# Two additions of a convolution–attention kernel: GpSimd tensor adds replaced by accumulating on-chip transfers that GpSimd issues

## The chip, the cores and the metric

One Trainium2 chip, one of its cores. The metric is the device time of one execution of the whole kernel in microseconds (us). Inputs come from the chip's memory (HBM) and the result goes back there; between them the data stay in the on-chip memory (SBUF) and in the matmul accumulators (PSUM).

## The reference

The input x has 16 images of 256 channels and 56x56 pixels, in float32. Two layers follow one another, each with a residual:

```python
# layer 0, on the group-normalised x
xq = sign(gn(x) + bias)
out = 0
for i, d in enumerate((1, 3, 5)):                      # dilations
    y = grouped_conv3x3(xq, binarised(w[i]), dilation=d) + cb[i] - move1[i]
    out = out + where(y >= 0, y, alpha[i] * y) + move2[i]   # PReLU
x = x + layer_norm_over_channels(out) * gamma + beta   # first residual
# layer 1, on the group-normalised x: local attention over 3x3 neighbours
q, k, v = gn(x) @ qkv_w.T + qkv_b
...
x = x + proj(softmax(q * k) * v)                       # second residual
```

Two additions in it matter here: the one that adds the third dilation's PReLU to the sum of the first two, and the first residual.

## The kernel before, in words

**Tiling.** The 256 channels are four groups (g) of 64. A tile's 128 partitions hold 64 channels twice, once for each half of the image. An image is worked on in two units (u = 0, 1), each of 2x7 rows of 56 pixels in either half, so that a unit's tile for one group has 128 partitions of 2x392 float32, 784 elements, 3136 bytes on each partition and 401,408 bytes (392 KB) in all. One image therefore has 8 such tiles, 24 convolutions (8 tiles, three dilations each), 8 additions of the third dilation and 8 additions of the first residual; 16 images have 128 of either addition.

**Convolution** (`conv`, from L634). TensorE makes 36 matmuls into a PSUM tile (L644); there are four such PSUM tiles for the whole kernel. PReLU is written as alpha*y + (1 - alpha)*relu(y). For the first dilation ScalarE writes the linear part to the tile `ct` (L663); for the second, VectorE adds it to `ct` (L673); for the third (`POOLED = (2,)`), ScalarE writes it to a tile of its own, `rl` (L670). Then, for each, ScalarE takes the relu in PSUM (L678), and VectorE adds its share to `ct` or to `rl` (L683). Last, for the third dilation alone, GpSimd adds `rl` to `ct` (L689). There are seven `ct` tiles but a single `rl` tile (`kind("rl", UNIT, 1)`, L415): the next third dilation's L670 can't start before the addition at L689 has read `rl`.

**Channel norm and first residual** (`channel_norm`, from L721). ScalarE squares `ct` (L727), TensorE sums over channels (L697), small VectorE and ScalarE operations make mean and root (L741 to L749), VectorE subtracts the mean (L755) and scales (L765). Then GpSimd adds `ct` to the input tile `xt` (L778), and ScalarE squares the new `xt` with a running sum (L782), for which it uses `ct` as its output. After the four groups of both units, `fold` makes the group norm of layer 1 out of these sums (matmul L514, then L526 and on) and folds it into the projection's weights (L803, L825); `qkv` (L862) uses them.

**Attention.** GpSimd multiplies q and k for nine shifts (L915), TensorE sums (L937), a softmax follows (L950 to L972), TensorE spreads the weights (L986), VectorE multiplies by v (L997) and GpSimd adds up the nine terms (L1010); TensorE projects (L1027), VectorE makes the second residual (L1037), and the tile is stored.

**Transfers.** All are issued by SyncE (SP): halves of images for the statistics and the signs (`xh`, L544), the units' inputs (`xt`, L1202), results (`out`, L1047), and small copies between the two halves of the partitions (`sgn`, L606 and L607). GpSimd issues none.

**Order.** Every operation is handed to `Plan.op` with what it reads and writes. A table (`ORDER`) gives each a place in time, and `Plan.emit` issues them in that order, as soon as what an operation depends on has been issued and its buffers are to be had. So each engine has a fixed order of instructions, in which convolutions of the next image are mixed with attention of the one before, and an engine whose next instruction waits does nothing else. `pool(...)` puts an operation on GpSimd. `either(...)` does so too, but moves those that `ON_VECTOR` lists to VectorE; of the two additions these are three of the last image's residual additions (`"scale1$": (1, 4, 10)`). The place in the order is the same for `pool` and `either`.

Of the kernel before, what the change touches and what calls it, by code (L numbers as in the profile page):

```python
# [11 lines left out]
ALU = mybir.AluOpType  # L12
# [281 lines left out]
class Plan:  # L294
# [16 lines left out]
    def op(self, engine, emit, r=(), w=(), hold=(), engines=()):  # L311


        k = self.noted.get((self.stage, self.image), 0)
        self.noted[self.stage, self.image] = k + 1
        if engines:
            emit = partial(emit, engines[k in ON_VECTOR.get(self.stage, ())])
        bufs = [k[0] if isinstance(k, tuple) else k for k in (*r, *w, *hold)]
        bufs = [k for k in dict.fromkeys(bufs) if isinstance(k, Buf)]
        o = Op(PERIOD * self.image + ORDER[self.stage][k], emit, bufs)  # L320
        for b in bufs:
            if not b.left and b.kind in self.queues:
                self.queues[b.kind].append(b)
            b.left += 1
        before = {}
        for k in r:
            for x in self.wrote.get(k, ()):
                before[id(x)] = x
        for k in w:
            for x in (*self.wrote.get(k, ()), *self.read.get(k, ())):  # L330
                before[id(x)] = x
        for k in r:
            self.read.setdefault(k, []).append(o)
        for k in w:
            self.wrote[k], self.read[k] = [o], []
        for x in before.values():
            x.after.append(o)
            o.wait += 1
        self.ops.append(o)
# [35 lines left out]
def preact_conv_attention(  # L375
# [16 lines left out]
    nc = tc.nc  # L392
# [84 lines left out]
    def pe(f, r, w, hold=()):  # L477
        op("PE", f, r, w, hold)

    def act(f, r, w):  # L480
        op("ACT", f, r, w)

    def dve(f, r, w):
        op("DVE", f, r, w)

    def pool(f, r, w):
        op("POOL", f, r, w)
# [4 lines left out]
    def either(f, r, w):  # L492

        op("POOL", f, r, w, engines=(nc.gpsimd, nc.vector))
# [139 lines left out]
    def conv(b, u, g, d, ct):  # L634

        dil = DIL[d]
        ps = Buf("ps")

        def products():
            for tap in range(9):  # L640
                c0 = PADC + (tap % 3 - 1) * dil
                for h, q in ((0, 0), (1, 1), (0, 1), (1, 0)):
                    r0 = PADC + q * XR + u * SR + (tap // 3 - 1) * dil
                    nc.tensor.matmul(  # L644
                        out=ps[q * GC : (q + 1) * GC, h, 0:SN],
                        lhsT=wconv[h * GC : (h + 1) * GC, g, d, tap, :],
                        rhs=sgn[g][h * GC : (h + 1) * GC, r0 : r0 + SR, c0 : c0 + W],
                        start=tap == 0,
                        stop=tap == 8,
                    )  # L650


        pe(products, [("sgn", g), ("halo", g), ("wconv", g, d)], [ps], [ct])

        def n():
            return ps[:, :, 0:SN]

        s = slice(d, d + 1)

        to = Buf("rl") if d in POOLED else ct  # L660
        if d == 0:
            act(
                lambda: nc.scalar.activation(  # L663
                    ct.tile, n(), AF.Identity, bias=mv2[:, g : g + 1], scale=asc[:, g, s]
                ),
                [ps, ("scales", g, d), "mv2"],
                [ct],
            )
        elif d in POOLED:
            act(lambda: nc.scalar.mul(to.tile, n(), asc[:, g, s]), [ps, ("scales", g, d)], [to])  # L670
        else:
            dve(
                lambda: nc.vector.scalar_tensor_tensor(ct.tile, n(), asc[:, g, s], ct.tile, ALU.mult, ALU.add),  # L673
                [ps, ("scales", g, d)],
                [ct],
            )
        act(
            lambda: nc.scalar.activation(n(), n(), AF.Relu, bias=cbi[:, g, s], scale=csc[:, g, s]),  # L678
            [("scales", g, d)],
            [ps],  # L680
        )
        dve(
            lambda: nc.vector.scalar_tensor_tensor(to.tile, n(), oalpha[:, g, s], to.tile, ALU.mult, ALU.add),  # L683
            [ps],
            [to],
        )
        if d in POOLED:
            either(
                lambda e: e.tensor_tensor(ct.tile, ct.tile, to.tile, ALU.add),  # L689
                [to],  # L690
                [ct])


    def lanes_sum(ps, bank, src, g):

        for i in range(NVB):
            nc.tensor.matmul(  # L697
                out=ps[i * LANES : (i + 1) * LANES, bank, 0:VB],
                lhsT=cm32,
                rhs=src[:, i // 2, i % 2 * VB : (i % 2 + 1) * VB],  # L700
                start=g == 0,
                stop=g == NG - 1,
            )
# [17 lines left out]
    def channel_norm(b, u, ct, xt, sums):  # L721

        ps = Buf("ps")
        for g in range(NG):
            plan.at(f"var{u}", b)
            sq = Buf("sq")
            act(lambda g=g, sq=sq: nc.scalar.activation(sq.tile, ct[g].tile, AF.Square), [ct[g]], [sq])  # L727

            def sum_of_both(g=g, sq=sq):
                lanes_sum(ps, 0, ct[g], g)  # L730
                lanes_sum(ps, 1, sq, g)

            pe(sum_of_both, [ct[g], sq], [ps])
        plan.at(f"root{u}", b)
        ms, t, s, r = (Buf("lv") for _ in range(4))


        mean, square = (lambda i=i: ps[:, i, 0:VB] for i in range(2))
        tt = nc.vector.tensor_tensor
        stt = nc.vector.scalar_tensor_tensor  # L740
        act(lambda: nc.scalar.copy(ms.tile, mean()), [ps], [ms])  # L741
        dve(lambda: tt(t.tile, mean(), ms.tile, ALU.mult), [ps, ms], [t])
        dve(lambda: stt(mean(), t.tile, -1.0, square(), ALU.mult, ALU.add), [t], [ps])
        dve(lambda: nc.vector.tensor_scalar(mean(), mean(), 0.0, EPS_LN, ALU.max, ALU.add), [], [ps])
        act(lambda: nc.scalar.activation(t.tile, mean(), AF.Ln), [ps], [t])
        act(lambda: nc.scalar.activation(square(), t.tile, AF.Exp, scale=-0.5), [t], [ps])
        act(lambda: nc.scalar.activation(s.tile, square(), AF.Square, scale=0.5**0.5), [ps], [s])
        dve(lambda: stt(t.tile, mean(), -1.0, s.tile, ALU.mult, ALU.mult), [ps, s], [t])
        dve(lambda: stt(r.tile, t.tile, 1.5, square(), ALU.add, ALU.mult), [t, ps], [r])  # L749
        plan.at(f"mean{u}", b)  # L750
        mb = Buf("ps")
        lanes_spread(mb, ms)
        for g in range(NG):
            dve(
                lambda g=g: nc.vector.tensor_tensor(ct[g].tile, ct[g].tile, mb[:, :, 0:SN], ALU.subtract),  # L755
                [mb],
                [ct[g]],
            )
        plan.at(f"root{u}", b)
        rb = Buf("ps")  # L760
        lanes_spread(rb, r)
        for g in range(NG):
            plan.at(f"scale{u}", b)
            dve(
                lambda g=g: nc.vector.scalar_tensor_tensor(  # L765
                    ct[g].tile,
                    ct[g].tile,
                    gam[:, g : g + 1],
                    rb[:, :, 0:SN],
                    ALU.mult,  # L770
                    ALU.mult,
                    accum_out=sums[:, g : g + 1],
                ),
                [rb],
                [ct[g], (sums, "sums")],
            )
            either(
                lambda e, g=g: e.tensor_tensor(xt[:, g], xt[:, g], ct[g].tile, ALU.add),  # L778
                [ct[g]],
                [(xt, g)])  # L780
            act(
                lambda g=g: nc.scalar.activation(  # L782
                    ct[g].tile,
                    xt[:, g],
                    AF.Square,
                    bias=bet[:, g : g + 1],
                    accum_out=sums[:, NG + g : NG + g + 1],
                ),
                [(xt, g)],
                [(sums, "squares"), ct[g]],  # L790
            )
# [420 lines left out]
    for b in range(NB):  # L1212
        sums = []
        xts = []
        for u in range(NU):
            ct = [Buf("ct") for _ in range(NG)]
# [134 lines left out]
```

## Time and profile before

| What | Value |
|---|---|
| median of 2 runs | 2101.8 us (2094.55 to 2109.05) |
| the profiled execution: its own time, its span | 2101.32 us, 2099.5 us |
| mean granted TensorE clock | 0.935 |
| busy: PE, VectorE (DVE), ScalarE (ACT), GpSimd (POOL) | 1798.0, 1625.2, 1292.8, 1508.4 us |
| one image in the middle of the run (884 to 1005 us from the span's start) | 121 us; PE 108.3, DVE 98.3, ACT 80.3, POOL 95.6 us busy |
| the addition at L689 | 128 on POOL, median 1857 ns |
| the addition at L778 | 125 on POOL, median 1862 ns; 3 on DVE |
| SP's queue of transfers | 211.68 MB, its packets 45.0% of 16 engines' span |

How to read it: times in a timeline are from the start of the span. A name such as "ct<-ct,rl" is what an instruction writes and reads. "idle before" is the time in which an engine stood still ahead of an instruction, and the arrow names what ended that wait. The chain of waits follows the work that ended last back through whatever released it.

### The profile page before, as it was taken

How to read it: one execution, taken by the hardware profiler on the slowest of the kernel's cores; microseconds unless marked ns; L12 is line 12 of the kernel's file. 1: busy time of each engine (PE TensorE's matmuls, PEld its weight loads, DVE VectorE, ACT ScalarE, POOL GpSimd, SP SyncE). 2: the span in 40 equal slices, each digit the busy share in tenths (PEclk: the TensorE clock that was granted, in tenths of full speed). 3: DMA queues.
4: the chain of work that ended last, by engine and by line, in shares of the span. 5: the costliest groups of instructions: out<-in, count | busy, mean ns of one | idle time of the engine just before them, and what ended most of it. 6: DMA issues, size and time to landing. Idle time of an engine off the chain costs nothing.

```text
span 2099.5 us, 71196 instructions
## 1 busy us (share of the span) xinstructions
PE 1798.0 (86%) x31770; PEld 906.3 (43%) x31770; DVE 1625.2 (77%) x2240; ACT 1292.8 (62%) x1733; POOL 1508.4 (72%) x884
## 2 busy tenths in 40 slices
PE   5667799898989989898989989898998989899694
PEld 4444254353535445353534435353443535344241
DVE  7565696968788696878879697877969687796876
ACT  6785575667667565767666576775757677463310
POOL 2233968878796887879597777968788786977714
PEclk8879999899999999999999999999999999999886
DMA  6760435535363654536364452637455353232212
GB/s 167 171 137 18 97 81 130 126 80 131 80 143 83 141 113 94 127 73 139 82 146 108 105 129 68 136 77 167 87 112 130 83 122 90 60 65 63 63 32 62
DMA packets 102420, 216.24 MB, mean 103 GB/s; under 512 B 10720, under 2 KB 84832, under 8 KB 102112
## 3 DMA queue, kind: packets, MB, share of 16 engines
q1 hardware_dynamic: 102112, 211.68, 45.0%
q8 instruction: 249, 4.08, 0.8%
q14 instruction: 59, 0.48, 0.1%
HBM read 154.85 MB, written 51.38 MB: 98 GB/s over the span
## 4 chain that ended last, share of the span: by engine, by line
PE 48%; DVE 27%; ACT 10%; issue 8%; POOL 4%; DMA 2%; SPq 0%; DVEq 0%; POOLq 0%; ACTq 0%
PE banks L644 16%; PE banks L862 12%; PE banks L937 7%; DVE m L997 5%; PE banks L986 4%; DVE xt L1037 4%; ACT xh L570 4%; PE banks L697 4%; DVE ct L765 3%; DVE ct L683 2%; ACT banks L678 2%; POOL m L1010 2%; DVE rl L683 2%; PE banks L1027 2%; DVE at L972 2%
## 5 line engine op out<-in xcount | busy, mean ns | idle before, releaser
L644 PE MATMUL banks<-sgn,wconv 64*64 64x392 bf16 x13824 | 674.3, 341 | 42.7 <-DVE rl L683 10.5
L1010 POOL TENSOR_TENSOR m<-m 128x784 f32<-128x784 f32 x252 | 469.7, 1864 | 169.1 <-DVE m L997 159.0
L644 PEld LDWEIGHTS <-wconv 64*64 64x64 bf16 x13824 | 441.5, 108 | 316.6 <-issue 144.4
L915 POOL TENSOR_TENSOR p<-qt,kt 128x784 f32<-128x784 f32 x273 | 473.1, 1768 | 108.8 <-PE banks L937 56.8
L678 ACT ACTIVATE banks<-banks,cbi,csc 128x784 f32<-128x784 f32 x384 | 373.0, 974 | 141.2 <-DVE ct L673 139.8
L689 POOL TENSOR_TENSOR ct<-ct,rl 128x784 f32<-128x784 f32 x128 | 237.9, 1859 | 247.0 <-DVE ct L683 99.9
L986 PE MATMUL banks<-at,wv 64*32 64x392 f32 x5120 | 315.6, 567 | 94.1 <-DVE m L997 49.9
L683 DVE SCALAR_TENSOR_TENSOR ct<-banks,oalpha,ct 128x784 f32<-128x784 f32 x256 | 262.0, 1028 | 84.9 <-ACT banks L678 82.7
L997 DVE TENSOR_TENSOR m<-banks,vt 128x784 f32<-128x784 f32 x288 | 274.6, 964 | 65.7 <-PE banks L986 59.3
L862 PE MATMUL banks<-xt,wf 64*64 64x392 f32 x3072 | 265.4, 495 | 3.9 <-DVE ct L755 3.9
L778 POOL TENSOR_TENSOR xt<-xt,ct 128x784 f32<-128x784 f32 x125 | 240.1, 1932 | 25.4 <-DVE ct L765 23.8
L937 PE MATMUL banks<-p,wk 32*64 32x392 f32 x4608 | 230.5, 499 | 11.7 <-POOL p L915 9.4
L673 DVE SCALAR_TENSOR_TENSOR ct<-banks,asc,ct 128x784 f32<-128x784 f32 x128 | 130.6, 1029 | 120.6 <-PE banks L644 117.1
L570 ACT ACTIVATE xh<-xh 128x1568 f32<-128x1568 f32 x120 | 180.9, 1508 | 7.2 <-DMA xh<-in_x 5.0
L986 PEld LDWEIGHTS banks<-at,wv 64*32 64x32 f32 x5120 | 67.3, 113 | 265.4 <-DVE m L997 106.1
L670 ACT ACTIVATE rl<-banks,asc 128x784 f32<-128x784 f32 x128 | 116.6, 911 | 103.6 <-POOL ct L689 59.1
L862 PEld LDWEIGHTS banks<-xt,wf 64*64 64x64 f32 x3072 | 114.3, 134 | 143.1 <-issue 131.0
L663 ACT ACTIVATE ct<-banks,mv,asc 128x784 f32<-128x784 f32 x128 | 128.3, 1003 | 49.1 <-PE banks L644 49.0
L683 DVE SCALAR_TENSOR_TENSOR rl<-banks,oalpha,rl 128x784 f32<-128x784 f32 x128 | 130.7, 1021 | 30.9 <-ACT banks L678 27.4
L1027 PE MATMUL banks<-m,wp 64*64 64x392 f32 x1024 | 116.2, 542 | 44.7 <-DVE xt L1037 24.7
L782 ACT ACTIVATE ct<-xt,pr 128x784 f32<-128x784 f32 x128 | 121.1, 947 | 42.0 <-POOL xt L778 34.3
L937 PEld LDWEIGHTS banks<-p,wk 32*64 32x64 f32 x4608 | 90.7, 131 | 118.4 <-issue 60.5
(111 smaller groups left out, 1961.8 us busy)
## 6 DMA issues: line engine op xcount, KB each, us to landing
xh<-in_x SPq DMA_DIRECT2D x248, 392.0 KB, 5.4
xt<-in_x SPq DMA_DIRECT2D x128, 392.0 KB, 7.0
out<-xt SPq DMA_DIRECT2D x128, 392.0 KB, 5.9
sgn<-sgn SPq DMA_DIRECT2D x128, 41.2 KB, 3.3
p<-in_w SPq DMA_DIRECT2D x12, 144.0 KB, 5.1
wq<-in_wqkv SPq DMA_DIRECT2D x1, 384.0 KB, 7.5
p<-in_wk_b SPq DMA_DIRECT2D x1, 320.0 KB, 6.9
p<-in_wk_c SPq DMA_DIRECT2D x1, 320.0 KB, 7.1
```

Of the source, the lines that this page charges most:

```text
L570: lambda func=func, col=col: nc.scalar.activation(inside(g) if b == 0 else image(xh), image(xh), func, accum_out=sums[:, col : col + 1]),
L644: nc.tensor.matmul(out=ps[q * GC : (q + 1) * GC, h, 0:SN], lhsT=wconv[h * GC : (h + 1) * GC, g, d, tap, :], rhs=sgn[g][h * GC : (h + 1) * ...
L678: lambda: nc.scalar.activation(n(), n(), AF.Relu, bias=cbi[:, g, s], scale=csc[:, g, s]),
L683: lambda: nc.vector.scalar_tensor_tensor(to.tile, n(), oalpha[:, g, s], to.tile, ALU.mult, ALU.add),
L689: lambda e: e.tensor_tensor(ct.tile, ct.tile, to.tile, ALU.add),
L778: lambda e, g=g: e.tensor_tensor(xt[:, g], xt[:, g], ct[g].tile, ALU.add),
L862: nc.tensor.matmul(out=ps[h * D : (h + 1) * D, q, 0:SN], lhsT=wf[q * GC : (q + 1) * GC, g, j, :], rhs=xt[q * GC : (q + 1) * GC, g, h, :], ...
L915: e.tensor_tensor(p.tile.rearrange("p x (r w) -> p x r w", w=W), _view(qt[:, 0, u * SN :], [(NU * SN + LANES, 2), (W, SR), (1, W)]), shift ...
L937: nc.tensor.matmul(out=ps[rt // 2][q * 64 : (q + 1) * 64, rt % 2, 0:n], lhsT=wk[r, j, :], rhs=rhs, start=s == 0, stop=s == 9,)
L986: nc.tensor.matmul(out=ps[rt * 32 : (rt + 1) * 32, q, 0:SN], lhsT=wv[q * 64 : (q + 1) * 64, j, :], rhs=at[q * 64 : (q + 1) * 64, rt, 0:SN] ...
L997: lambda j=j, m=m, ps=ps: nc.vector.tensor_tensor(m.tile.rearrange("p x (r w) -> p x r w", w=W), _view(ps[:, 0, :], [(512, 2), (W, SR), (1 ...
L1010: lambda e, m=m, acc=acc: e.tensor_tensor(acc.tile, acc.tile, m.tile, ALU.add),
```

## The change

The third dilation's addition and the first residual's addition are no longer GpSimd instructions that read two tiles and write one. Each is a transfer, issued by GpSimd on its own queue, from `rl` into `ct` and from `ct` into `xt`, which adds what it brings to what is there. The lists of what they read and write are the same, and so is the order of the program. Whoever uses `ct`, `rl` or `xt` next waits for the transfer's completion instead of for GpSimd's instruction. The three residual additions that were on VectorE in the last image become such transfers too.

```diff
@@ -685,10 +685,11 @@
         if d in POOLED:
-            either(
-                lambda e: e.tensor_tensor(ct.tile, ct.tile, to.tile, ALU.add),
+            pool(
+                lambda: nc.gpsimd.dma_start(out=ct.tile, in_=to.tile, accum_op=ALU.add),
                 [to],
-                [ct])
+                [ct],
+            )
@@ -774,10 +775,11 @@
-            either(
-                lambda e, g=g: e.tensor_tensor(xt[:, g], xt[:, g], ct[g].tile, ALU.add),
+            pool(
+                lambda g=g: nc.gpsimd.dma_start(out=xt[:, g], in_=ct[g].tile, accum_op=ALU.add),
                 [ct[g]],
-                [(xt, g)])
+                [(xt, g)],
+            )
```

## The prediction

> **What bounds the kernel now.** I read the page from the top: busy shares, chain of waits, costliest groups, then DMA issues.
>
> ```profile
> PE 1798.0 (86%) x31770; PEld 906.3 (43%) x31770; DVE 1625.2 (77%) x2240; ACT 1292.8 (62%) x1733; POOL 1508.4 (72%) x884
> ...
> PE 48%; DVE 27%; ACT 10%; issue 8%; POOL 4%; DMA 2%; SPq 0%; DVEq 0%; POOLq 0%; ACTq 0%
> ...
> L689 POOL TENSOR_TENSOR ct<-ct,rl 128x784 f32<-128x784 f32 x128 | 237.9, 1859 | 247.0 <-DVE ct L683 99.9
> ...
> L778 POOL TENSOR_TENSOR xt<-xt,ct 128x784 f32<-128x784 f32 x125 | 240.1, 1932 | 25.4 <-DVE ct L765 23.8
> ...
> L670 ACT ACTIVATE rl<-banks,asc 128x784 f32<-128x784 f32 x128 | 116.6, 911 | 103.6 <-POOL ct L689 59.1
> ```
>
> No single engine sets the time: TensorE leads, VectorE follows, and the chain passes from one to the other. GpSimd is 72% busy but has 4% of the chain. Adding up the chain's pieces by line, L689 has 14.8 us of it and L778 5.6 us, 20.4 of 2099.5. The last row matters most: ScalarE's L670 waits 59.1 us for the very addition that is changed, because there is one `rl`.
>
> Next, the timelines of ScalarE and GpSimd in one image of the middle (121 us, from 884). ScalarE:
>
> ```profile
> 893.66 0.91 ACT L670 ACTIVATE rl<-banks,asc 128x784 f32<-128x784 f32 x1 [1.10 <-POOL ct L689]
> ...
> 899.24 0.91 ACT L670 ACTIVATE rl<-banks,asc 128x784 f32<-128x784 f32 x1 [2.23 <-POOL ct L689]
> ...
> 906.11 0.91 ACT L670 ACTIVATE rl<-banks,asc 128x784 f32<-128x784 f32 x1
> ...
> 914.87 0.91 ACT L670 ACTIVATE rl<-banks,asc 128x784 f32<-128x784 f32 x1
> ```
>
> GpSimd:
>
> ```profile
> 891.77 1.85 POOL L689 TENSOR_TENSOR ct<-ct,rl 128x784 f32<-128x784 f32 x1
> 893.60 3.80 POOL L1010 TENSOR_TENSOR m<-m 128x784 f32<-128x784 f32 x2
> 897.36 1.85 POOL L689 TENSOR_TENSOR ct<-ct,rl 128x784 f32<-128x784 f32 x1
> 899.16 3.67 POOL L778 TENSOR_TENSOR xt<-xt,ct 128x784 f32<-128x784 f32 x2
> 902.77 1.87 POOL L689 TENSOR_TENSOR ct<-ct,rl 128x784 f32<-128x784 f32 x1
> ```
>
> L689 ends at 893.63, L670 starts at 893.66; L689 ends at 899.21, L670 starts at 899.24. So `rl` is a ring: L670, relu L678, L683, L689, next L670. Slack from an addition's end to the next L670, for the image's eight: 0.03, 0.03, 1.47, 0.82, 29.89, 5.70, 0.04 and 11.47 us. Five of eight are tight. The pattern repeats: over the whole run 43 of 127 slacks are under 0.2 us and 80 under 5 us. In the first stretch (884 to 915) VectorE is busy 29.5 of 31 us, and lines of DVE make up most of the chain there.
>
> **What the Trainium skill says.** (1) "DMA: Bandwidth & Descriptors", section "Anatomy of one DMA": a GpSimd-issued transfer takes about 2.0 us plus bytes/436e3; for 401,408 bytes 2.92 us. The trace has no such transfer, only SP's; a 41.2 KB one would be 2.1 us by this, and takes 3.3, and the large ones take twice 2.9:
>
> ```profile
> xh<-in_x SPq DMA_DIRECT2D x248, 392.0 KB, 5.4
> xt<-in_x SPq DMA_DIRECT2D x128, 392.0 KB, 7.0
> out<-xt SPq DMA_DIRECT2D x128, 392.0 KB, 5.9
> sgn<-sgn SPq DMA_DIRECT2D x128, 41.2 KB, 3.3
> ```
>
> (2) Same page, "Rules for kernel authors": an accumulating DMA reads its destination and writes it later, and another access must wait for its semaphore. So it moves more than a copy, and `rl` is free only at landing. No run so far shows it. (3) "Perfetto Trace Analysis", "DMA Instruction — SWDGE (GPSIMD)": GpSimd's own cores write the descriptors, and the profiler's end of the instruction is the end of that, not of the data. So GpSimd is let go earlier than the data land; how early the trace doesn't show. (4) "SBUF — State Buffer", "Who interferes with whom": a VectorE instruction with two SBUF inputs contends with a GpSimd one that reads SBUF. In the trace only a few L778 suffer (median 1.86, longest 2.80 us beside L962), so removing the adds gives VectorE almost nothing: I take 0.
>
> **The change, part by part.** Let L be the time from the point at which GpSimd could start the add to the landing, and D = L - 1.86 what each dependent waits longer.
>
> *Removed:* 128 x 1.857 + 125 x 1.862 = 470 us of GpSimd time and 3 x 1.06 us of VectorE's. *Added:* 256 issues on GpSimd. Their price is not in the trace: at least 0.1 us, at most about the add itself (1.86). I take 1.2, from the page's 1 us to first byte, so GpSimd saves 0.66 x 253 = 167 us of busy time. What of that is on the path? L689 and L778 have 20.4 us of the chain; products and sums behind them (L915, L1010) wait mostly for DVE and PE. I credit 20 us, about all of the two lines' share; zero and 40 are the ends.
>
> *L.* Low end 2.9 (the page's fit, though for a copy). High end 10: two passes over the data behind a burst of SP's. The nearest row is `out<-xt`, same size, SBUF source, landing in 5.9 us; an accumulating transfer to SBUF spares the HBM receipt, but reads twice and has slower descriptor making. I take **5.9, D = 4.04**.
>
> *The ring.* Each L670 is late by D less its slack. Queued behind it on ScalarE are its own L678, which VectorE's L683 needs, and L594 or L782; VectorE, in order, then stalls with L755 and L765 of the other unit behind it, and TensorE when none of its four PSUM tiles comes free. In the first stretch the four cycles run one after another with VectorE full, so delays add: 4.01 + 4.01 + 2.57 + 3.22 = 13.81 us. The seventh (986.58) is tight as well; its VectorE partner L683 at 990.23 has 0.95 us to spare after L678, and VectorE is then full to 1006: 3.05 us. The others are covered by slacks of 5.70 and more; that cover ends at L = 7.6.
>
> *First residual.* After L778 comes L782 on ScalarE. At 963.30 it starts 0.04 us after its add; behind it are the statistics L570 and L663, where ScalarE's next wait is 1.02 us: 4.04 - 0.04 - 1.02 = 2.98 us. Two have slacks of 14 us and more. One (slack 1.57, 2.47 us late) is hidden by the 0.49 and 4.61 us that ScalarE idles next. Four lie inside the ring's stretch, within about 1 us of the L670 that is late anyway: 0. If that cover fails, up to 4 us an image.
>
> *Others.* `ct` of L689 is next read by L727 13 to 70 us later: 0. The DMA engines: 256 x 0.4014 = 102.8 MB. 45.0% moved 211.68 MB, so +22 points as a copy, +44 if the second read counts: 67 to 89%. SP's loads share with it; between 945 and 968 the share is already 0.76. I put that into L, not beside it. The program's order on SP doesn't change.
>
> *Sum.* Per image 13.81 + 3.05 + 2.98 = 19.84 us, which is 6D - 4.4 for D from 1.5 to 5.7. Times 16: 317 us. Less 20: +297. On the profiled execution 2099.5 + 297 = 2397 us of span, 2398 with the 1.8 us around it; its time (2101.32) is 0.5 us from the median (2101.8). **2400 us, 14% slower.** First and last image are counted like the others; they are looser, and this is the coarsest step.
>
> **Rivals.**
> - *The transfer itself is slow* (accumulation at half rate, or queued behind SP's bursts): L of 8 to 10. Then 32.9 to 46.9 us an image, 2099.5 + 526 - 20 = 2606 to 2830. For it: two reads, 0.76 busy in bursts. Against: digits of 0 in the DMA row between bursts, and the ring's stretch has a share of 0.48.
> - *Mild:* L of 3.3 to 4, D 1.44 to 2.14: with the same sum 4.6 to 8.4 us an image, 2153 to 2215. For it: SBUF on both sides, 128 rows of 3136 bytes. Against: the 3.3 us of the small copies.
> - *Not slower: the landing is about as soon as the add's end.* Place: the two tight ring cycles 893 and 899. At L = 2.5 they cost 2 x 0.61 x 16 = 19.5 us, which the 20 us credit just pays: that is the point that decides. At L = 2.9 it's 38 - 20: 2120 us. At L = 2.0: 2085. To pass 2% faster, 42 us, GpSimd's relief must also move L1010 and L915, which have 43.0 and 17.2 us of the chain. Against: no transfer of the trace lands under 2.4 us, whatever its size.
> - *GpSimd isn't let go* (writing descriptors takes it 2 us or more each): no credit, and L grows by the 0.8 us over my 1.2, so D = 4.84, 24.6 us an image, 2099.5 + 394 = 2494 us. For it: three descriptors a row instead of two. Against: nothing in this trace, either way.
>
> **How the numbers follow.** Likeliest (L 4 to 8, 2215 to 2606): 0.64. Slow: 0.13. GpSimd not let go: 0.03 beside those, with L inside the likeliest's. Mild: 0.12. Not slower: 0.08. About 2% is what a measurement of this kernel can tell from no change. The last case splits into 0.03 faster and 0.05 within 2%; the rest is slower, 0.92. The range for 8 in 10: from 2160 (L = 3.4) to 2760 (L = 9.4).
>
> **What would show it.** L670's idle time with the transfer as its releaser, not 59.1 us but some 128 x 2.5 us, and the whole in proportion. Landing of the new issues: 5.9 us median means the sum was right, below 3 the third rival, above 8 the first. GpSimd's busy time near 1508 - 478 = 1030 us (issues are not counted as busy). PE, DVE and ACT busy times the same, their shares down. VectorE in the first stretch idle <-ACT L678. Wrong if landings are long yet L670 rarely waits, or if GpSimd's queue grows a wait of its own ahead of L1010 or L915.

## The result, and the profile after

The changed kernel takes 2421.98 us (median of 2 runs, 2417.6 to 2426.37) against 2101.8: a ratio of 1.152, 95% interval 1.133 to 1.172. It is slower by 320 us. The prediction was 2400 us, with 2160 to 2760 around it.

From the page of the changed kernel (lines after L689 have moved by one or two: L779 issues the residual's transfer, L784 is the square after it, L988, L999 and L1012 are the attention's L986, L997 and L1010). First busy times, then groups: busy time and mean ns of one, then idle time ahead and what ended most of it.

```profile
PE 1880.2 (78%) x31770; PEld 935.7 (39%) x31770; DVE 1614.5 (67%) x2237; ACT 1295.4 (54%) x1733; POOL 1258.8 (52%) x887
...
L689 POOL DMA_DIRECT2D ct<-rl x128 | 120.0, 937 | 586.4 <-DVE rl L683 282.3
...
L670 ACT ACTIVATE rl<-banks,asc 128x784 f32<-128x784 f32 x128 | 116.5, 911 | 309.8 <-DMA ct<-rl 260.4
...
L784 ACT ACTIVATE ct<-xt,pr 128x784 f32<-128x784 f32 x128 | 121.2, 947 | 173.4 <-DMA xt<-ct 105.8
...
L779 POOL DMA_DIRECT2D xt<-ct x128 | 114.9, 917 | 84.3 <-DVE ct L766 75.3
```

L670 waited 59.1 us for GpSimd's addition; now it waits 260.4 us for the landing of its transfer (some 320 were forecast). VectorE and ScalarE do the same work as before (1625.2 and 1292.8 us then), so the time went into waits. GpSimd is down from 1508.4 to 1258.8 us, and gained nothing from it. (This run's chain of waits can be followed back over only 9% of the span, so nothing rests on it.)

The queues and the issues' time to landing (from the start of GpSimd's or SP's issue until the transfer reports completion), on the same page; q1 is SP's queue and q0 GpSimd's:

```profile
q1 hardware_dynamic: 102112, 211.68, 38.5%
q0 software_dynamic: 36864, 102.78, 23.2%
...
ct<-rl POOLq DMA_DIRECT2D x128, 392.0 KB, 5.4
...
xt<-ct POOLq DMA_DIRECT2D x128, 392.0 KB, 6.9
```

Medians of 5.4 and 6.9 us, where the tensor adds took 1.86. Now the ring of the one `rl` in one image. ScalarE's timeline:

```profile
1043.61 0.91 ACT L670 ACTIVATE rl<-banks,asc 128x784 f32<-128x784 f32 x1 [8.44 <-DMA ct<-rl]
...
1051.27 0.92 ACT L670 ACTIVATE rl<-banks,asc 128x784 f32<-128x784 f32 x1 [4.31 <-DVE xt L1039]
...
1061.51 0.91 ACT L670 ACTIVATE rl<-banks,asc 128x784 f32<-128x784 f32 x1
...
1073.45 0.92 ACT L670 ACTIVATE rl<-banks,asc 128x784 f32<-128x784 f32 x1 [1.73 <-DMA ct<-rl]
```

GpSimd's timeline of the same stretch; its instruction ends when it has issued, not when the data are there:

```profile
1034.35 0.89 POOL L689 DMA_DIRECT2D ct<-rl  x1
...
1046.75 0.88 POOL L689 DMA_DIRECT2D ct<-rl  x1 [7.24 <-DVE rl L683]
...
1054.41 0.86 POOL L689 DMA_DIRECT2D ct<-rl  x1 [3.02 <-DVE rl L683]
...
1069.35 0.86 POOL L689 DMA_DIRECT2D ct<-rl  x1 [8.39 <-PE banks L644]
```

The first is issued at 1034.35 and lands at 1043.5, and L670 starts at 1043.61. The second lands at 1051.2, and L670 starts at 1051.27. (The line names VectorE there, but its L1039 isn't what `rl` waits for: the landing falls within 0.1 us of the start.) Between, GpSimd stands idle for 7.24 us for VectorE, VectorE for ScalarE, ScalarE for the landing: all engines wait for one transfer.

The eight steps from one L670 to the next, as means over the 6th to the 13th image, with the median landing of the transfer that closes each:

| step | before, us | after, us | more | landing, us |
|---|---|---|---|---|
| 1 | 9.56 | 16.91 | +7.35 | 9.3 |
| 2 | 5.57 | 7.71 | +2.14 | 4.4 |
| 3 | 7.70 | 10.61 | +2.91 | 6.9 |
| 4 | 8.55 | 11.29 | +2.74 | 4.2 |
| 5 | 39.34 | 38.47 | -0.87 | 4.0 |
| 6 | 18.75 | 21.26 | +2.51 | 9.9 |
| 7 | 13.18 | 17.46 | +4.28 | 7.1 |
| 8 | 18.63 | 18.51 | -0.12 | 3.9 |
| an image | 121.3 | 142.2 | +20.9 | |

### The profile page after: what moved, and what is told of

It is laid out like the page before. It is cut to its first block, busy times and chain, and to the rows that moved or that the text cites. A ratio compares the mean times of both kernels' runs of the same rounds, so it can differ in the third digit from the quotient of the medians.

```text
span 2415.8 us, 71612 instructions
## 1 busy us (share of the span) xinstructions
PE 1880.2 (78%) x31770; PEld 935.7 (39%) x31770; DVE 1614.5 (67%) x2237; ACT 1295.4 (54%) x1733; POOL 1258.8 (52%) x887
## 3 DMA queue, kind: packets, MB, share of 16 engines
q1 hardware_dynamic: 102112, 211.68, 38.5%
q0 software_dynamic: 36864, 102.78, 23.2%
## 5 line engine op out<-in xcount | busy, mean ns | idle before, releaser
L644 PE MATMUL banks<-sgn,wconv 64*64 64x392 bf16 x13824 | 734.0, 363 | 196.3 <-DVE rl L683 121.7
L644 PEld LDWEIGHTS <-wconv 64*64 64x64 bf16 x13824 | 459.8, 115 | 505.1 <-issue 303.3
L1012 POOL TENSOR_TENSOR m<-m 128x784 f32<-128x784 f32 x252 | 470.8, 1868 | 330.3 <-DVE m L999 296.6
L988 PE MATMUL banks<-at,wv 64*32 64x392 f32 x5120 | 325.5, 587 | 132.4 <-DVE m L999 47.4
L689 POOL DMA_DIRECT2D ct<-rl x128 | 120.0, 937 | 586.4 <-DVE rl L683 282.3
L683 DVE SCALAR_TENSOR_TENSOR ct<-banks,oalpha,ct 128x784 f32<-128x784 f32 x256 | 262.4, 1030 | 197.4 <-ACT banks L678 195.7
L999 DVE TENSOR_TENSOR m<-banks,vt 128x784 f32<-128x784 f32 x288 | 275.8, 966 | 74.5 <-PE banks L988 69.0
L670 ACT ACTIVATE rl<-banks,asc 128x784 f32<-128x784 f32 x128 | 116.5, 911 | 309.8 <-DMA ct<-rl 260.4
L784 ACT ACTIVATE ct<-xt,pr 128x784 f32<-128x784 f32 x128 | 121.2, 947 | 173.4 <-DMA xt<-ct 105.8
L988 PEld LDWEIGHTS banks<-at,wv 64*32 64x32 f32 x5120 | 69.8, 115 | 307.7 <-DVE m L999 104.0
L779 POOL DMA_DIRECT2D xt<-ct x128 | 114.9, 917 | 84.3 <-DVE ct L766 75.3
L1039 DVE SCALAR_TENSOR_TENSOR xt<-banks,prb,xt 128x784 f32<-128x784 f32 x128 | 128.6, 1028 | 15.8 <-PE banks L1029 15.2
```

The lines of the kernel that those rows point to most:

```text
L644: nc.tensor.matmul(out=ps[q * GC : (q + 1) * GC, h, 0:SN], lhsT=wconv[h * GC : (h + 1) * GC, g, d, tap, :], rhs=sgn[g][h * GC : (h + 1) * ...
L988: nc.tensor.matmul(out=ps[rt * 32 : (rt + 1) * 32, q, 0:SN], lhsT=wv[q * 64 : (q + 1) * 64, j, :], rhs=at[q * 64 : (q + 1) * 64, rt, 0:SN] ...
L999: lambda j=j, m=m, ps=ps: nc.vector.tensor_tensor(m.tile.rearrange("p x (r w) -> p x r w", w=W), _view(ps[:, 0, :], [(512, 2), (W, SR), (1 ...
L1012: lambda e, m=m, acc=acc: e.tensor_tensor(acc.tile, acc.tile, m.tile, ALU.add),
```

## Experiments

The main theory is the prediction's ring: L670 waits for the landing that frees the one `rl`. The rivals: the residual's landings, the load on the DMA engines, or the adding itself. Each comparison is with runs of the kernel before on the same chip.

### One half of the change at a time

Only the PReLU's addition is a transfer (e2). Against the changed kernel:

```diff
-            pool(
-                lambda g=g: nc.gpsimd.dma_start(out=xt[:, g], in_=ct[g].tile, accum_op=ALU.add),
+            either(
+                lambda e, g=g: e.tensor_tensor(xt[:, g], xt[:, g], ct[g].tile, ALU.add),
...
```

> Only the third dilation's addition is a transfer; the residual is GpSimd's tensor add again. Ring theory: 13.81 + 3.05 us an image remain, less about 10 of relief, so 2340 to 2380 us. Rival (the residual's landings weigh as much): below 2270 us.

2339 us, 1.115 (1.113 to 1.117), +243 us: half a us below what the ring theory gave, and far above the rival. ScalarE's wait is the ring's (us in total, times, longest):

```profile
ACT rl L670 <- DMA ct<-rl: 299.1, 67, 9.6
```

In the table's terms steps 1 to 4 are longer by 7.19, 2.23, 0.46 and 1.88 us than before and the seventh by 4.24; the sixth is not longer (-0.12).

Only the residual's addition is a transfer (e3). Against the changed kernel:

```diff
-            pool(
-                lambda: nc.gpsimd.dma_start(out=ct.tile, in_=to.tile, accum_op=ALU.add),
+            either(
+                lambda e: e.tensor_tensor(ct.tile, ct.tile, to.tile, ALU.add),
...
```

> Only the first residual's addition is a transfer; the PReLU's is GpSimd's tensor add again. Ring theory: 2.98 us an image, less about 10, so 2120 to 2160 us. Rival (residual's landings weigh as much): above 2240 us.

2243 us, 1.070 (1.068 to 1.071), +147 us. The expectation was wrong, and by three times: the time is where the rival had put it. The square of the residual on the page of the kernel before, then two groups of this kernel's page:

```profile
L782 ACT ACTIVATE ct<-xt,pr 128x784 f32<-128x784 f32 x128 | 121.1, 947 | 42.0 <-POOL xt L778 34.3
...
L783 ACT ACTIVATE ct<-xt,pr 128x784 f32<-128x784 f32 x128 | 120.8, 946 | 211.9 <-DMA xt<-ct 105.9 <-DVE ct L765 46.7 <-DVE xt L1038 37.7
L670 ACT ACTIVATE rl<-banks,asc 128x784 f32<-128x784 f32 x128 | 116.5, 910 | 100.3 <-POOL ct L689 58.9 <-PE banks L644 40.4 <-POOL wf L804 0.8
```

L670 waits for GpSimd's add 58.9 us, as before the change; the loss is ahead of the square of the residual (L782 before, L783 here), which waited 34.3 us for GpSimd then and waits 105.9 us for landings now. In the table's terms steps 3, 4 and 6 are longer by 4.87, 1.38 and 2.37 us. The sum of the two halves is 390 us and both together lose 320: some 70 us lie under one another. So the residual's landings in the ring's stretch cost so little in the changed kernel only because the ring was late as well.

### A second rl tile

```diff
-    kind("rl", UNIT, 1)
+    kind("rl", UNIT, 2)
```

In the changed kernel (e1):

> The changed kernel with two rl tiles instead of one. Ring theory (L670 waits for the landing that frees the one rl): nearly all of L670's 260 us of waiting for ct<-rl goes, and with it about 16.9 of the 19.8 us an image that the prediction summed, so 2140 to 2200 us. Rival (the residual's landings and the DMA engines' load set the time): stays above 2300 us.

2284 us, 1.089 (1.087 to 1.092), +188 us. Neither expectation holds: the second tile takes back some 130 of 320 us, not the 220 or more of the ring theory. ScalarE's waits in this kernel:

```profile
ACT ct L784 <- DMA xt<-ct: 90.2, 58, 15.2
ACT rl L670 <- DMA ct<-rl: 61.5, 14, 6.4
```

The ring's wait fell from 260.4 to 61.5 us; the residual's stayed. To see the ring without the residual, the same second tile in e2's kernel, with the PReLU's transfers alone (e11):

> Only the third dilation's addition is a transfer, and there are two rl tiles. Ring theory: with the second tile nothing waits for these landings, so e2's 2339 us falls to 2100 to 2150 us. Rival (the PReLU's transfers cost in another way too: ct's readers, DMA load): above 2200 us.

2142 us, 1.022 (1.019 to 1.024), +47 us, in the range that the ring theory gave: one more tile takes e2's +243 down to +47. Not all waiting is gone, though: L670 still waits 67.9 us for landings, and the square of `ct` (L728) 37.9. And 47 + 147 is 194, close to the 188 of both with two tiles: with the ring open, the two halves add.

The same edit in the kernel before (e5):

> The kernel before with two rl tiles. It takes away L670's 59 us of waiting for the addition. VectorE is busy 29.5 of 31 us in that stretch, so most of it should only move the wait: 2075 to 2100 us. Rival (the ring already sets the time before the change): below 2060 us.

2110 us, 1.003 (1.002 to 1.005): 8 us slower, above what was expected. The 59 us of L670's waits were worth nothing there, because the wait moved to TensorE, for which L670 had waited 44.4 us:

```profile
ACT rl L670 <- PE banks L644: 80.8, 60, 5.5
...
ACT rl L670 <- POOL ct L689: 3.0, 1, 3.0
```

That VectorE, nearly full in that stretch, stands behind this is likely, but was not tried by itself.

### What the landing is made of

A plain copy in place of the accumulation (e4):

```diff
-                lambda: nc.gpsimd.dma_start(out=ct.tile, in_=to.tile, accum_op=ALU.add),
+                lambda: nc.gpsimd.dma_start(out=ct.tile, in_=to.tile),
...
-                lambda g=g: nc.gpsimd.dma_start(out=xt[:, g], in_=ct[g].tile, accum_op=ALU.add),
+                lambda g=g: nc.gpsimd.dma_start(out=xt[:, g], in_=ct[g].tile),
```

> The changed kernel with both transfers as plain copies (they overwrite ct and xt instead of adding, so both additions are left out). If adding costs a second read of the destination, landings come about 1 us sooner and the time falls to 2310 to 2370 us. If adding in flight is free against a copy, 2400 to 2440 us and the same landings. If adding is the main cost, below 2200 us.

2313 us, 1.104 (1.101 to 1.106), as expected. Its queue and issues:

```profile
q0 software_dynamic: 20480, 102.78, 13.7%
...
ct<-rl POOLq DMA_DIRECT2D x128, 392.0 KB, 3.6
```

In the quiet steps (4, 5 and 8) a copy lands in 2.6 us and an accumulation in 4.2, 4.0 and 3.9. The same 102.78 MB keep the DMA engines busy for 13.7% of 2309.8 us (316) as a copy and 23.2% of 2415.8 (560) with addition: 1.8 times. The adding in flight is so about a third of the loss (217 against 320 us more than before, from different chips), not all of it.

Short rows (e7):

```diff
-                lambda: nc.gpsimd.dma_start(out=ct.tile, in_=to.tile, accum_op=ALU.add),
+                lambda: nc.gpsimd.dma_start(out=ct[:, 0, 0:128], in_=to[:, 0, 0:128], accum_op=ALU.add),
```

and likewise `xt[:, g, 0, 0:128]` from `ct[g][:, 0, 0:128]`:

> The changed kernel with both transfers cut to 128 of 784 columns (the other columns' additions are left out): 64 KB instead of 392. If a landing is a fixed time plus a queue behind SP's loads, quiet landings fall from about 4.2 to 2.5 to 3 us, the one beside the xt loads stays at 6 us or more, and the time is 2170 to 2260 us. If the transfer's own bytes make the long landings, all are below 4 us and the time is below 2150 us.

2240 us, 1.067 (1.064 to 1.071), as the first of the three expectations has it. Quiet landings are 2.3 to 2.7 us, the one of step 1 is still 7.2 us, and those of steps 6 and 7 6.1 and 5.6. With a sixth of the bytes nearly half of the loss remains. ScalarE's wait on this kernel's `rl`:

```profile
  DMA ct<-rl: 150.9, 36
```

More loads (e8), after the four of each xt load, into two tiles `spare` of their own:

```diff
+            for i in range(2):
+                nc.sync.dma_start(
+                    out=spare[i], in_=x[b, i * P : (i + 1) * P, 0 : 2 * SR].rearrange("c r w -> c (r w)")
+                )
```

> The changed kernel with two more loads of 392 KB, into tiles that nobody reads, issued by SP right after each xt load. If the first addition of the ring lands late because it shares the DMA engines with the xt load (9.2 us against 4.2 in quiet), it now takes 11 to 13 us and the time rises by 30 to 70 us over 2422. If sharing isn't the reason, its landing stays at 9.2 and the time within 15 us.

2462 us, 1.173 (1.170 to 1.177). Step 1's landing goes from 9.3 to 10.7 us, a bit less than expected; the time rises by 40 us, though the intervals of the two ratios overlap by a little.

How SP's loads make this landing long shows in the changed kernel's trace. Step 1's transfer is issued 1.7 to 3.7 us after the four xt loads (1030.6 to 1032.6), which land until 1041.1, and it follows at 1043.5. The DMA view of the window from its issue to 1039, when the loads are nearly through (packets, MB, share of 16 engines):

```profile
q1 hardware_dynamic: 643, 0.96, 107.7%
```

And from there to its landing:

```profile
q0 software_dynamic: 144, 0.40, 46.1%
q1 hardware_dynamic: 111, 0.15, 18.0%
```

For 4.65 us the DMA engines are full of SP's packets and none of the transfer's 144 starts. As a median over the 6th to the 13th image, step 1's first packet starts 5.0 us after the issue, against 1.45 us in the quiet steps 4 and 5; with e8's two more loads it is 6.6, and with only 64 KB (e7) 4.8. GpSimd's own part was no longer than elsewhere (0.89 us). So the transfer is not just slowed by sharing: it starts late, with 64 KB as with 392. Why its packets don't get in between SP's, no run shows.

Not every long landing is made by SP's loads alone. In e2, where the residual's transfers are gone and SP's loads stay, step 1 still lands in 9.0 us, but step 3 in 3.9 instead of 6.9 and step 6 in 5.8 instead of 9.9. In these two steps the residual's transfers count, which GpSimd issues shortly before on the same queue (at 1050.53 ahead of 1054.41; at 1117.35 and 1119.67 ahead of 1120.25). Step 7 falls from 7.1 to 5.2; what makes the difference there is open.

### What the relief of GpSimd is worth

The kernel before, with both additions cut to 8 columns (e6):

```diff
-                lambda e: e.tensor_tensor(ct.tile, ct.tile, to.tile, ALU.add),
+                lambda e: e.tensor_tensor(ct[:, 0, 0:8], ct[:, 0, 0:8], to[:, 0, 0:8], ALU.add),
...
-                lambda e, g=g: e.tensor_tensor(xt[:, g], xt[:, g], ct[g].tile, ALU.add),
+                lambda e, g=g: e.tensor_tensor(xt[:, g, 0, 0:8], xt[:, g, 0, 0:8], ct[g][:, 0, 0:8], ALU.add),
```

> The kernel before with both additions cut to 8 of 784 columns on GpSimd (the other columns' additions are left out): GpSimd is relieved of nearly all of the 478 us and the results come 1.7 us sooner. It is the most that relieving GpSimd can give. Prediction's credit of about 20 us, plus the ring's shorter cycles: 2050 to 2085 us. Rival (relief also moves the products and sums behind): below 2040 us.

2078 us, 0.989 (0.987 to 0.991), 23 us less, as expected. In its groups L689 costs 205 ns instead of 1859, and L670 hardly waits for it:

```profile
L670 ACT ACTIVATE rl<-banks,asc 128x784 f32<-128x784 f32 x128 | 116.4, 909 | 84.3 <-PE banks L644 82.6 <-PE banks L986 0.9 <-POOL ct L689 0.7
```

That is about the most that a faster way to do these additions can bring in this order of the program. Could transfers get some of it, where their result is wanted late? In the kernel before, four of an image's sixteen additions became transfers (e9; `late` is (4, 7) for the PReLU and (1, 2) for the residual):

```diff
+    def add(e, what, late, to, of):
+        n = seen[what]
+        seen[what] = n + 1
+        if n % 8 in late:
+            nc.gpsimd.dma_start(out=to, in_=of, accum_op=ALU.add)
+        else:
+            e.tensor_tensor(to, to, of, ALU.add)
```

> The kernel before, but four additions an image are transfers: those whose result is used more than 11 us later (5th and 8th PReLU addition, 2nd and 3rd residual addition of an image, counted in the order on GpSimd); the other twelve stay tensor adds. Ring theory: no landing is waited for, GpSimd saves about 1 us each, so 2080 to 2105 us. Rival (transfers cost by loading the DMA engines, wherever they are): above 2125 us.

2113 us, 1.005 (1.003 to 1.006): half a per cent slower, a little outside what was expected and far from the rival. GpSimd's busy time fell by 71 us for nothing.

But one of the four is not late. The next L670 leaves the eighth PReLU addition 11 us, yet the `ct` that it writes is read at once. In the kernel before:

```profile
992.27 1.89 POOL L689 TENSOR_TENSOR ct<-ct,rl 128x784 f32<-128x784 f32 x1
...
994.84 1.61 ACT L727 ACTIVATE sq<-ct 128x784 f32<-128x784 f32 x2
```

The square of `ct` follows the addition's end by 0.7 us here, and by 0.03 in five of eight images. In e9 this square (L737 there) waits for the landing in 15 images:

```profile
ACT sq L737 <- DMA ct<-rl: 32.4, 15, 5.9
```

So e9 does not show that late transfers gain nothing; whether the other three alone would gain was not tried. The same four with two `rl` tiles (e10):

> As e9, with two rl tiles: 2060 to 2095 us if the two small gains add; no better than e9 if VectorE sets that stretch.

2117 us, 1.007 (1.004 to 1.009): no better than e9, with the eighth addition's landing in the way as well. No version with transfers that was run beats the kernel before.

## Why the prediction was right, step by step

**The ring** (13.81 us for steps 1 to 4, 3.05 for the seventh) is the cause of most of it, and e2 and e11 show it. In the changed kernel the four came out at 7.35 + 2.14 + 2.91 + 2.74 = 15.14 us, part of steps 3 and 4 being the residual's, and the seventh at 4.28. In e2, which has the ring without the residual's transfers, the four are 7.19 + 2.23 + 0.46 + 1.88 = 11.76 us, the seventh 4.24. "Delays add" held: with e2's own landings (9.0, 4.5, 3.9 and 4.2 us) in place of 5.9, the prediction's sum for the four gives 11.81. For the seventh it gives 2.35 (landing 5.2), and the rest of the 4.24 is open.

**L = 5.9 us for every landing** was near the mean (6.5 us over all 256) and wrong as a model. A landing takes about 4 us in quiet (3.9 to 4.2) or just ahead of SP's loads (4.4, step 2), and 7 to 10 behind or beside other transfers. Step 1's cost was taken as 4.01 and is 7.35, step 2's as 4.01 and is 2.14. The working had put sharing "into L"; it belonged to single transfers, by what SP and GpSimd itself had in flight at each. The row that was used as nearest, a store to HBM, had no claim to be it; that its 5.9 us came near the mix is luck, and so in part is the closeness of the sum, in which step 1 is too small by 3.34 us and step 2 too large by 1.87.

**The residual** (2.98 us an image, four landings in the ring's stretch at 0) is right in the changed kernel: step 6 shows 2.51, and nothing in e2, where the residual is no transfer. As a statement on the residual by itself it fails, as e3 shows: 147 us, not 48. The prediction named the cover ("the L670 that is late anyway") and priced its loss at up to 4 us an image; it is 6.25 (steps 3 and 4 of e3).

**The steps priced at nothing.** Step 6's landing takes 9.9 us, past the 7.6 at which its cover was said to end, and still comes 3.5 us before the next L670 (1129.3 against 1132.78), since everything ahead of that L670 has slipped too. The square of `ct` (L728) does wait 24.6 us for landings in all, which the working had at 0: it read L727 as 13 to 70 us behind every addition, and overlooked the eighth, behind which it comes within 0.7 us.

**Two smaller readings** were off without moving the forecast. The rival "not slower" had no transfer landing under 2.4 us in the kernel before; 45 of the 128 small `sgn` copies do, the soonest in 1.8. And at D = 1.44 the working's own sum gives 4.3 us an image for "mild", not 4.6, so 2148 us instead of 2153.

**The credit of 20 us** for GpSimd's relief was well sized: 23 us with nearly all of it gone. In the changed kernel it is not to be seen apart. The issue was taken as 1.2 us and is 0.87 (median at L689). It counts as busy, so GpSimd shows 1258.8 us and not the 1030 that were forecast.

**PE's busy time "the same"** was wrong. It rose by 82 us for the same 31770 instructions, and the mean granted clock fell from 0.935 to 0.883. The changed kernel by windows (columns after the stretch: its length, busy us and instructions of PE, of its weight loads, DVE, ACT and POOL, then clock, DMA share, GB/s), the first while step 1's landing is awaited, the second behind it:

```profile
1038.00:1046.50 8.50, 0.83 (x18) 0.56 (x17) 1.47 (x3) 2.90 (x3) 1.51 (x1) 0.76 0.48 90
1046.50:1050.00 3.50, 3.49 (x44) 2.20 (x43) 3.46 (x5) 0.45 (x1) 1.74 (x2) 0.61 0.56 105
```

PE stands idle for 7.67 us, from 1038.8 on. The same view gives a clock of 0.50 from 1042.4 to 1049.2 and of 1.00 from 1049.3 on, and PE's next 36 convolution matmuls take 3.00 us instead of 1.74. In the kernel before the clock is 1.00 all through the first stretch (884 to 915). The Trainium skill has this in "TensorE: Matmul & The Clock Gate", Part 1: after an idle window of about 3.4 us the array runs at half clock until it has been busy for as long. The trace agrees on the half clock, which comes about 3.6 us after PE's last work; it ends 2.7 us after PE's return, sooner than the page has it. So this wait cost about 1.3 us more than it lasted. How much of the 82 us lies on the path was not tried; it is a term that the sum lacked.

**The DMA engines' share** was put at 67 to 89% and is 62% (38.5 + 23.2), in a longer span. By time the transfers keep the engines busy 560 us, toward the low end of the 460 to 920 that +22 to +44 points of the old span are: an accumulation costs 5.5 us per MB, SP's traffic 4.4.

**First and last image** were counted like the others, which was called the coarsest step, and it came out. From the first L670 of the first image to that of the second it is 105.8 us instead of 78.7, and from the last image's first L670 to the end 262.7 instead of 248.8: together 41.0 us more, as for two images of the middle (41.8). But 16 x 20.9 would be 334 us, and the two spans differ by 316: the 2nd to the 5th image, the 14th and the 15th lose only 18.2 us each as a mean.

The rivals "mild" and "not slower" fall with landings of 3.9 us at the least and half of the eight near 7 and above; "slow" (8 to 10) holds for two landings in eight. "GpSimd isn't let go" is out: 0.87 us each.

## What to carry to other kernels

Price a transfer that replaces an instruction by its time to landing at the place where it stands, with what all queues, its own too, have in flight there, and not by a mean; then ask of each buffer that it holds, source and destination alike, how long its next user can wait. Look for the buffer with a single copy first: a second `rl` was worth 196 us with the PReLU's transfers alone, some 130 with both transfers, and nothing in the kernel before. And a cost that is hidden under another delay comes out when that delay is cured: measure halves alone, not only the whole.

## What the runs showed of the hardware

An accumulating transfer of 392 KB within SBUF lands 3.9 to 4.2 us after GpSimd starts to issue it (medians of steps 4, 5 and 8) with nothing else in flight; a plain copy 2.6, and 64 KB with addition 2.3 to 2.4. Issued 1.7 to 3.7 us after four loads of 392 KB from HBM on SP's queue, the large one takes 9.3 us and the small one 7.2: its first packet starts 5.0 and 4.8 us after the issue, instead of 1.45, while SP's packets keep the engines full. Transfers that GpSimd has just issued on its own queue lengthen a landing too: 6.9 and 9.9 us with them, 3.9 and 5.8 without. Issuing one holds GpSimd for 0.87 us, a copy for 0.54.
